# Picked k and v move to the edge values' PSUM bank, and the units of picks run on across groups

## The chip, the cores and the metric

The kernel runs on one core of a Trainium2 chip. The metric is device time in microseconds (us), from one launch. Five engines work beside each other, each through its own instructions in order: PE (TensorE, matmuls; its weight loads are shown as PEld), DVE (VectorE), ACT (ScalarE), POOL (GpSimd, which here issues the gathers) and SP (SyncE, which here issues the other DMAs). They wait for each other by semaphores. [...]

## The reference

6,250 nodes with 64 values each, 206,250 edges sorted by destination, one edge attribute of 64 values for each edge:

```python
Qh = (x @ Wq.T + bq).reshape(n, H, D)          # H = 4 heads, D = 16
Kh = (x @ Wk.T + bk).reshape(n, H, D)
Vh = (x @ Wv.T + bv).reshape(n, H, D)
Ee = (edge_attr @ We.T + be).reshape(-1, H, D)
score = (Kh[src] * Qh[dst] * (1.0 / np.sqrt(D)) * Ee).sum(-1)
score = jnp.exp(jnp.clip(score, -5.0, 5.0))
msg = Vh[src] * score[..., None]
wV = jax.ops.segment_sum(msg, dst, num_segments=n)
out = layernorm(x + wV)
```

So each edge needs k and v of its source, q of its destination and its own edge values; then messages are summed by destination.

## The kernel before

**Tiles and groups.** 128 edges are a tile, 8 tiles a group, and there are 202 groups (`NG`). A prologue (about the first 100 us) makes the tables of q, k and v in HBM. Then the loop `for g in range(NG + 1)` does one group in each iteration, with the parts of several groups in flight: edge values of group g+3, queries of g+2, the transposed product of g+1, and scores and messages of g.

**k and v of the sources.** Most tiles get k and v by an indirect DMA from the table (`gather_kv`, L295, on POOL, one for each tile). For the last two tiles of four groups out of five they are picked by PE instead. A batch is four such tiles, 512 edges: PE multiplies x by one-hot columns, in 13 units (`UNITS`). A unit is four matmuls of 128 x 512, two into each of the PSUM banks `px[0]` and `px[1]`; the thirteenth is two. So a batch is 50 matmuls (`picks`). There are 78 batches, and both banks belong to one batch at a time: they accumulate over its 13 units. The one-hot columns come from DVE (`hots`, L696) for pieces of two units; for three pieces of seven, DVE makes them in bf16 and ACT widens them (`widened`, L707). They are made in the iteration ahead of the one that uses them, into six buffers.

**The end of a batch.** When its last unit is done, DVE masks both banks into SBUF (`picked`, `xs[0]` and `xs[1]`, L722 and L723). Only then may the next batch's first unit write `px`. In the iteration after, ACT fills the bank `rooms` with the bias (`biased_kv`, L733), PE multiplies `xs` by the weights into it (`picked_kv`, 8 products, 16 records), and ACT copies it to the tiles' places among k and v (`place_kv`, L739, two copies). `rooms` is the bank `qq`, into which PE also writes the queries of a group (`queries`) and which DVE's `terms` (L769) reads.

**The edge values' bank.** PE writes the edge values of group g+3 into `ee` at the end of iteration g (`edges`, 2 matmuls, the group `room<-et,we_sb` of the profile); ACT adds the bias and copies them to SBUF early in iteration g+1 (`biased`, L755). `ee` is one half of a PSUM tile `room` of two banks. The other half holds `pa`, the sums of the messages (PE `sums`, the group `room<-msg`; read by DVE's `add`, L900), and `folded` (PE `fold_blocks`, read by `add_blocks`, L957).

**Which iteration does what.** Batches take three and two iterations in turn (`LENGTHS = [3, 2]`), so the loop repeats after five. I call them places 1 to 5: g = 1, 6, 11, ... is place 1. A batch's units never pass its own iterations: places 1 to 3 do 4, 4 and 5 units of one batch, places 4 and 5 do 6 and 7 units of the next. A batch ends in places 3 and 5 (`READY`), and `picked` stands at the very end of DVE's work there; biases, products and copies of k and v follow in places 4 and 1.

**Order within an iteration**, by engine, as written out by hand:

- PE: two units of picks; the transposes of g+1 (`turn`, L775, needs `terms` of g+1); then `queries` of g+2, or in places 4 and 1 `picked_kv` instead; the rest of the units with the sums (every other iteration) and folds between them; in places 4 and 1 `queries` only here, behind `place_kv`; `edges`.
- DVE: `products` (L806, L808), `terms` of g+1, `add`, `add_blocks`, one piece's `hots`, `message` (L830), the other pieces, the one-hot rows of the sums (L792), `take` (L850), in places 3 and 5 `picked`, then some layer norm.
- ACT: `weigh` (L813, L815), in places 4 and 1 `biased_kv`, `biased` of g+2, a copy of the messages (L844), widening, the one-hot columns of the queries (L272, L278), in places 4 and 1 `place_kv`; `sources` (L257 and L258, with L259 on DVE) turns a batch's source numbers into what `hots` compares.
- SP: the loads, with `fetch_sources` (L252, 256 KB into one buffer) among those of edges, queries and keys.
- POOL: 6 or 8 gathers, each behind a mark in PE's order.

What follows are the functions that the change touches, with the line numbers of the profile.

## Time and profile before

| | |
|---|---|
| median of 3 runs | 1998.6 us (1994.48 to 2001.87) |
| the profiled execution | 2019.47 us, span 2017.7 us |
| PE busy | 1738.5 us, 86% of the span |
| DVE busy | 1486.0 us, 74% |
| ACT busy | 1328.1 us, 66% |
| POOL busy | 1255.5 us, 62% |
| granted TensorE clock, mean | 0.932 |
| picks on PE | 3900 matmuls, 1143.6 us busy, 115.5 us idle before them |
| gathers on POOL | 1260, mean 965 ns |

Read it so: no engine is busy all the time, and PE is busiest. Matmuls overlap in their pipeline, so PE's busy time is not time at its peak rate, and the mean of one matmul is longer than the distance from its start to the next one's. The granted clock is the share of full speed at which TensorE was allowed to run. Idle time counts only on the engine that sets the pace; the rows that tell for whom PE waited are therefore the first to read.

### The profile page before, as it was taken

Reading aid. Unit: us, or ns where it says so; the run is one execution under the profiler, and the core shown is the slowest. Engines: PE = TensorE matmul, PEld = TensorE weight load, DVE = VectorE, ACT = ScalarE, POOL = GpSimd, SP = SyncE. Lnnn points to the kernel's source line nnn. Section 1 sums busy time; section 2 is a strip of 40 time slices with the busy share of each in tenths; the row PEclk is TensorE's granted clock in tenths of the full one; section 3 lists DMA queues with packets and bytes.
Section 4 is the critical chain, followed back from the end, with each engine's and each line's share of the span. In section 5 each row is a group of like instructions: output and inputs, shape, how many; then the busy total and the mean of one; then the engine's idle time right before and its main releaser. Section 6 shows DMA issues by size and latency. Waiting matters only on the chain.

```text
span 2017.7 us, 25692 instructions
## 1 busy us (share of the span) xinstructions
PE 1738.5 (86%) x7993; PEld 1259.1 (62%) x7993; DVE 1486.0 (74%) x2650; ACT 1328.1 (66%) x2047; POOL 1255.5 (62%) x1310
## 2 busy tenths in 40 slices
PE   6569989888888898979888989888888988889995
PEld 6346666666666665657566666666666666656664
DVE  5457777777777686878777777778777777678786
ACT  3456676676766676767667667667766667577674
POOL 6566666666666665666666666666666666666441
PEclk9789999999999998999899999999989999999996
DMA  6523333333333333333333333333333333333320
GB/s 178 190 90 114 100 103 103 98 97 100 93 108 101 91 102 88 102 115 99 93 97 92 107 104 93 104 90 103 101 88 114 104 95 104 97 93 98 97 71 20
DMA packets 116116, 203.70 MB, mean 101 GB/s; under 512 B 54784, under 2 KB 56425, under 8 KB 115855
## 3 DMA queue, kind: packets, MB, share of 16 engines
q1 hardware_dynamic: 73932, 116.94, 19.0%
q0 software_dynamic: 41600, 83.97, 14.7%
q10 hardware_dynamic: 436, 1.04, 0.2%
q8 instruction: 65, 1.06, 0.2%
q14 instruction: 83, 0.68, 0.1%
HBM read 194.25 MB, written 7.59 MB: 100 GB/s over the span
## 4 chain that ended last, share of the span: by engine, by line
PE 63%; DVE 16%; issue 7%; ACT 6%; another core or an unknown queue 4%; DMA 2%; POOL 1%; DVEq 0%; SPq 0%; ACTq 0%; POOLq 0%
PE pick L744 37%; PE room L744 10%; PE qq L744 10%; PE qe L775 4%; DVE hot L696 3%; DMA kv<-kv_tab,src_i 2%; DVE score L808 2%; DVE prod L806 1%; DVE qe L830 1%; DVE x L722 1%; DVE term L769 1%; POOL kv L295 1%; ACT kv L739 1%; DVE msg L850 1%
## 5 line engine op out<-in xcount | busy, mean ns | idle before, releaser
L295 POOL DMA_INDIRECT kv<-kv_tab,src_i x1260 | 1216.2, 965 | 708.8 <-issue 277.1
L744 PE MATMUL pick<-hot,parts 128*128 128x512 f32 x3900 | 1143.6, 436 | 115.5 <-DVE x L722 79.5
L744 PEld LDWEIGHTS pick<-hot,parts 128*128 128x128 f32 x3900 | 742.3, 198 | 418.8 <-issue 167.8
L696 DVE TENSOR_TENSOR hot<-from,still 128x1024 fp32r<-128x1024 bf16 x231 | 280.3, 1213 | 0.6 <-ACT from L257 0.6
L707 ACT ACTIVATE hot<-thin 128x1024 fp32r<-128x1024 bf16 x234 | 245.4, 1049 | 19.4 <-remote 19.3
L769 DVE TENSOR_TENSOR term<-eb,qq 128x512 f32<-128x512 f32 x202 | 137.3, 680 | 137.2 <-PE qq L744 98.1
L755 ACT ACTIVATE eb<-room,be_col 128x512 f32<-128x512 f32 x202 | 137.1, 679 | 148.2 <-DVE still L900 50.4
L744 PE MATMUL room<-et,we_sb 128*128 128x512 f32 x404 | 226.2, 642 | 7.5 <-ACT eb L755 6.2
L844 ACT ACTIVATE msg<-qe 128x512 fp32r<-128x512 f32 (+1 forms) x206 | 123.2, 598 | 157.5 <-DVE qe L830 74.4
L278 ACT ACTIVATE to<-to,one_p 126x1024 bf16<-126x1024 bf16 x198 | 225.7, 1140 | 0.1
L272 ACT ACTIVATE to<-kb,minus_row 126x1024 bf16<-126x1024 uint8 x198 | 225.2, 1137 | 0.0
L813 ACT ACTIVATE score<-score,five_p 128x32 f32<-128x32 f32 x203 | 64.1, 316 | 235.4 <-DVE score L808 144.6
L775 PE MATMUL qe<-ident,term 128*128 128x128 f32 x806 | 135.5, 294 | 58.9 <-DVE term L769 39.4
L775 PEld LDWEIGHTS qe<-ident,term 128*128 128x128 f32 x806 | 104.0, 151 | 111.9 <-DVE term L769 55.8
L744 PE MATMUL qq<-w,x 128*128 128x128 f32 x1248 | 165.8, 288 | 5.0 <-issue 3.6
L806 DVE TENSOR_TENSOR prod<-kv,qe 128x512 f32<-128x512 f32 x203 | 137.0, 675 | 43.1 <-remote 38.3
L830 DVE SCALAR_TENSOR_TENSOR qe<-weight,kv 128x512 f32<-128x512 f32 x200 | 139.8, 699 | 35.1 <-ACT weight L815 22.3
L722 DVE SCALAR_TENSOR_TENSOR x<-odd,upper,pick 128x512 f32<-128x512 int32 x77 | 57.3, 744 | 144.7 <-PE pick L744 115.2
L744 PEld LDWEIGHTS qq<-w,x 128*128 128x128 f32 x1248 | 155.6, 202 | 12.9 <-issue 8.0
L696 DVE TENSOR_TENSOR thin<-from,still 128x1024 bf16<-128x1024 bf16 x231 | 157.1, 680 | 0.0
L808 DVE TENSOR_REDUCE score<-prod 128x32 f32<-128x512 f32 x203 | 138.5, 682 | 7.0
L850 DVE TENSOR_TENSOR msg<-qe,msg 128x512 fp32r<-128x512 f32 x194 | 132.2, 681 | 2.9 <-ACT msg L844 1.4
(166 smaller groups left out, 1490.5 us busy)
## 6 DMA issues: line engine op xcount, KB each, us to landing
et<-in_eT SPq DMA_DIRECT2D x100, 512.0 KB
kb<-key_tab SPq DMA_DIRECT2D x101, 252.0 KB
kv<-kv_tab,src_i POOLq DMA_INDIRECT x1260
srcs<-in_src_rows SPq DMA_DIRECT2D x78, 256.0 KB
qw<-q_tab SPq DMA_DIRECT2D x202, 15.8 KB
kv_tab<-kv_sb SPq DMA_DIRECT2D x4, 640.0 KB
q_tab<-q SPq DMA_DIRECT2D x5, 480.0 KB
out<-y SPq DMA_DIRECT2D x2, 512.0 KB
```

The costliest lines, as they stand in the source:

```text
L272: nc.scalar.activation(TO[g][:, :n, :], KB.pop(g)[:, :n * P].rearrange("p (j e) -> p j e", j=n), AF.Square, bias=minus_row3[:3 * W])
L278: nc.scalar.activation(TO[g][:, :n, :], TO[g][:, :n, :], AF.Relu, bias=one_p[:3 * W], scale=-1.0)
L295: return nc.gpsimd.indirect_dma_start(out=kv_of(g)[:, j, :], out_offset=None, in_=kv_tab[:, :], in_offset=bass.IndirectOffsetOnAxis(ap=src ...
L696: nc.vector.tensor_tensor(to.rearrange("p b (a c) -> p b a c", c=2), pairs((FROM if hi < UNITS else OVER)[m])[:, None].to_broadcast(shape) ...
L707: nc.scalar.activation(*THIN.pop(0), AF.Copy)
L744: mark.append(nc.tensor.matmul(*aps, **kw))
L769: nc.vector.tensor_mul(TERM[g][:, :n], EB.pop(g)[:, :n], qq[:, :n])
L775: nc.tensor.transpose(qe[g % 2][:, 2 * k:2 * k + 2, :], TERM[g][:, k, :], ident)
L806: nc.vector.tensor_mul(prod, kv_of(g)[:, lo:hi, :C], qe[g % 2][:, lo:hi, :])
L808: nc.vector.tensor_reduce(SCORE[g], prod.rearrange("p g (h d) -> p g h d", h=H), axis=AX.X, op=OP.add)
L830: nc.vector.scalar_tensor_tensor(to.rearrange("p g (h d) -> p g h d", h=H), WEIGHT.pop(g)[:, :, :, None].to_broadcast([P, n, H, D]), LEAST ...
L850: nc.vector.tensor_sub(part_of(g, 1)[1], left, part)
```

## The change

Three things change together.

1. **The bank of k and v.** `ee` and `room` become two tiles of one bank each, in place of one tile of two banks. `rooms`, where k and v of a batch are made, is now `ee` and no longer `qq`. So `queries` of g+2 takes its place in the middle of every iteration, and it is `edges` of g+3 that comes behind `place_kv` in places 4 and 1. `biased_kv` moves behind `biased` on ACT, since it now overwrites what `biased` reads.
2. **Units run on.** The units of all batches are one stream, cut in 4, 6, 6, 4, 6 for places 1 to 5 (one more in the very first). A batch's end lies within an iteration: in place 3 the first two units are its last ones (`head`), and four of the next batch follow; in place 5 the first five are its last ones, and one of the next batch follows. PE's order there is: the head (with `turn` behind the head of two, or after the second unit of the head of five), `queries`, sums and folds, `edges`, and only then the next batch's units. `picked` moves forward on DVE: in place 3 it stands behind `add` and `add_blocks`, ahead of the `hots` and of `message`; in place 5 behind `message` and all `hots`, ahead of the one-hot rows and `take`.
3. **Sources.** `fetch_sources` and `sources` come one iteration earlier, since the next batch's first pieces are needed earlier. In the iteration of a batch's end, its `sources` for the batch after next follow `picked`.

Work is neither added nor removed: as many matmuls, copies and DMAs as before.

```diff
--- before.py
+++ after.py
@@ -97,13 +97,27 @@
 READY = [begin(m + 1) - 1 for m in range(LAST)]
 
 
+FLOW = 4, 6, 6, 4, 6
+STREAM = [(m, p, u) for m in range(LAST) for p, piece in enumerate(PIECES) for u in range(*piece)]
+UPTO = [0] * (LEAD + 1)
+for g in range(LEAD, NG):
+    UPTO.append(UPTO[-1] + FLOW[(g - LEAD) % len(FLOW)] + (g == LEAD))
+assert UPTO[NG] >= len(STREAM)
+assert all(UPTO[r] < (m + 1) * UNITS <= UPTO[r + 1] for m, r in enumerate(READY))
+
+
+def units_of(g):
+
+    return STREAM[UPTO[g]:UPTO[g + 1]] if g < NG else []
+
+
 def pieces_of(g):
 
-    for m in range(LAST):
-        if BEGIN[m] <= g <= READY[m]:
-            n, k = READY[m] - BEGIN[m] + 1, g - BEGIN[m]
-            return [(m, p) for p in range(len(PIECES) * k // n, len(PIECES) * (k + 1) // n)]
-    return []
+    return [(m, p) for m, p, u in units_of(g) if u == PIECES[p][0]]
+
+
+SOURCES = {LEAD: 1, **{r: m + 2 for m, r in enumerate(READY)}}
+FETCHES = {r - 1: m + 2 for m, r in enumerate(READY)}
 
 
 PICKED = [(r + k, r + k + 1) for r in READY for k in [min(4, NG - 2 - r - 1)]]
@@ -663,17 +677,17 @@
             nc.tensor.transpose(col, row_b[:, 0:1].to_broadcast([P, P]), ident_b)
             nc.tensor.transpose(still[:, C:C + UNITS].bitcast(BF16),
                                 half_b[:2 * UNITS].to_broadcast([2 * UNITS, P]), ident_b[:2 * UNITS, :2 * UNITS])
-            room = fixed.tile([P, 2, 4 * P], F32, name="room")
-            ee = room[:, 0].rearrange("p (i e) -> p i e", e=P)
-            pa = room[:, 1, :2 * PA]
-            folded = room[:, 1, 2 * PA:2 * PA + 2 * C].rearrange("p (b c) -> p b c", c=C)
+            ee = fixed.tile([P, G // 2, P], F32, name="ee")
+            room = fixed.tile([P, 4 * P], F32, name="room")
+            pa = room[:, :2 * PA]
+            folded = room[:, 2 * PA:2 * PA + 2 * C].rearrange("p (b c) -> p b c", c=C)
             sum_ = still[:, 2 * P:2 * P + C]
             px = [fixed.tile([P, 4 * P], F32, name=f"pick{k}") for k in range(2)]
             xs = [accp.tile([P, 4 * P], F32, name=f"x{k}") for k in range(2)]
             qq = fixed.tile([P, G // 2, P], F32, name="qq")
             qe = [fixed.tile([P, G, C], F32, name=f"qe{k}") for k in range(2)]
 
-            rooms = qq.rearrange("p i e -> p (i e)").rearrange("p (j c) -> p j c", j=BATCH)
+            rooms = ee.rearrange("p i e -> p (i e)").rearrange("p (j c) -> p j c", j=BATCH)
 
             def pairs(ap):
 
@@ -1013,7 +1027,9 @@
             widened()
             for g in range(NG + 1):
                 now, before = g < NG, g > 0
-                todo, ahead = [(m, p, u) for m, p in pieces_of(g) for u in range(*PIECES[p])], pieces_of(g + 1)
+                todo, ahead = units_of(g), pieces_of(g + 1)
+                ending = READY.index(g) if g in READY else None
+                head = [one for one in todo if one[0] == ending]
                 going, where = [], []
                 if g == 0:
                     going = alone(lots(4))
@@ -1025,8 +1041,8 @@
                     nc.sync.dma_start(dst_c[:, :min(KEYS, T - t)], dst[:, t:min(t + KEYS, T)])
                 if g % LG == 0 and g + 3 * LG < NG:
                     fetch_edges(g // LG + 3, work, 3)
-                if g + 1 in BEGIN[1:]:
-                    fetch_sources(BEGIN.index(g + 1) + 1, work)
+                if g in FETCHES:
+                    fetch_sources(FETCHES[g], work)
                 if g + 4 < NG:
                     fetch_queries(g + 4)
                 if g % 2 == 0 and g + 6 < NG:
@@ -1052,10 +1068,15 @@
                     add(s)
                 if g - 1 in FOLDS:
                     add_blocks(FOLDS[g - 1])
+                if 0 < len(head) <= 3:
+                    for one in head:
+                        picks(*one)
+                        where.append(mark[-1])
+                    picked(ending)
+                if g + 2 < NG:
+                    biased(g + 2)
                 if g - 1 in READY:
                     biased_kv(READY.index(g - 1))
-                if g + 2 < NG:
-                    biased(g + 2)
                 for piece in ahead[:1]:
                     hots(*piece)
                 if now:
@@ -1082,31 +1103,48 @@
                         short += [lambda lo=lo: sums(s, slice(lo, lo + 4)) for lo in range(0, G, 4)]
                     else:
                         short.append(lambda: sums(s))
-                for k in range(max(len(todo), 3)):
+                for k, one in enumerate(head if len(head) > 3 else []):
+                    picks(*one)
+                    where.append(mark[-1])
+                    if k == 1 and g + 1 < NG:
+                        turn(g + 1)
+                if head:
+                    if len(head) <= 3 and g + 1 < NG:
+                        turn(g + 1)
+                    if g + 2 < NG:
+                        queries(g + 2)
+                    while short:
+                        short.pop(0)()
+                    if g + 3 < NG:
+                        edges(g + 3)
+                    if len(head) > 3:
+                        picked(ending)
+                    for one in todo[len(head):]:
+                        picks(*one)
+                        where.append(mark[-1])
+                for k in range(0 if head else max(len(todo), 3)):
                     for one in todo[k:k + 1]:
                         picks(*one)
                         where.append(mark[-1])
                     if k == 1:
                         if g + 1 < NG:
                             turn(g + 1)
+                        if g + 2 < NG:
+                            queries(g + 2)
                         if g - 1 in READY:
                             picked_kv(READY.index(g - 1))
                             place_kv(READY.index(g - 1))
-                        elif g + 2 < NG:
-                            queries(g + 2)
-                    if k in (2, 4) and short and g not in READY:
+                    if k in (2, 4) and short:
                         short.pop(0)()
                 while short:
                     short.pop(0)()
-                if g + 2 < NG and g - 1 in READY:
-                    queries(g + 2)
-                if g + 3 < NG:
+                if g + 3 < NG and not head:
                     edges(g + 3)
                 where.append(mark[-1])
                 if g + 4 < NG:
                     onehot_rows_rest(g + 4)
-                if g in BEGIN:
-                    sources(BEGIN.index(g) + 1, *from_odd())
+                if g in SOURCES:
+                    sources(SOURCES[g], *from_odd())
                 for i, lot in enumerate(going):
                     gather((lot, where[i * len(where) // len(going)]))
                 for h in ([g] if g < NG - 3 else []) + ([g + 1] if NG - 4 <= g < NG - 1 else []):
@@ -1122,8 +1160,6 @@
                         widen(s)
                 if parted:
                     take(g, 0)
-                if g in READY:
-                    picked(READY.index(g))
                 if done:
 
                     while closed < B - 2 and summed[closed] <= g:
```

## The prediction

> **What bounds the kernel now.** I read the page first: span, busy times, and the chain that ended last.
>
> ```profile
> span 2017.7 us, 25692 instructions
> PE 1738.5 (86%) x7993; PEld 1259.1 (62%) x7993; DVE 1486.0 (74%) x2650; ACT 1328.1 (66%) x2047; POOL 1255.5 (62%) x1310
> PE 63%; DVE 16%; issue 7%; ACT 6%; another core or an unknown queue 4%; DMA 2%; POOL 1%; DVEq 0%; SPq 0%; ACTq 0%; POOLq 0%
> L295 POOL DMA_INDIRECT kv<-kv_tab,src_i x1260 | 1216.2, 965 | 708.8 <-issue 277.1
> ```
>
> PE sets the pace, but only 63% of the chain is its work. So I ask for whom PE waits, and read the view of waits (line, releaser: us in total, times, longest), PE's rows first, then four of DVE and ACT.
>
> ```profile
> PE pick L744 <- DVE x L722: 79.5, 23, 6.0
> PE qq L744 <- ACT kv L739: 44.0, 32, 4.4
> PE qe L775 <- DVE term L769: 39.4, 22, 12.3
> PE pick L744 <- issue: 35.1, 37, 2.5
> ...
> DVE x L722 <- PE pick L744: 115.2, 42, 5.1
> DVE term L769 <- PE qq L744: 98.1, 50, 5.1
> ...
> ACT eb L755 <- DVE still L900: 50.4, 20, 6.5
> ACT eb L755 <- DVE y L957: 40.1, 13, 7.4
> ```
>
> The first row is the end of a batch: PE has nothing to do until DVE has emptied `px`. Next I cut the loop into cycles of five iterations, at the ends of place 5's edge matmuls. The windows' columns are us, busy us (and instructions) of PE, PEld, DVE, ACT and POOL, granted clock, DMA share, GB/s. The first row is all 39 cycles, the others single ones.
>
> ```profile
> 103.60:1971.70 1868.10, 1647.44 (x7684) 1191.61 (x7683) 1404.04 (x2413) 1265.25 (x1898) 1186.21 (x1231) 0.94 0.34 99
> 977.80:1024.40 46.60, 41.80 (x200) 31.14 (x199) 35.21 (x61) 32.68 (x49) 30.44 (x32) 0.93 0.37 108
> 1838.10:1887.00 48.90, 41.97 (x197) 30.05 (x197) 36.85 (x67) 32.80 (x49) 31.31 (x33) 0.97 0.37 110
> 1887.00:1928.70 41.70, 40.33 (x198) 29.53 (x197) 35.81 (x61) 31.58 (x48) 14.04 (x15) 1.00 0.26 77
> ```
>
> A cycle takes 1868.1 / 39 = 47.9 us, PE is busy for 42.2 of it, and the clock is below full speed. One late cycle has next to no stall and a clock of 1.00: 41.7 us. It also has half the gathers (15 against 33), so it shows what PE can do, not what the whole kernel can. Then the timeline around an end of a batch in place 3 (start, us, what, idle time before it), with the same work undisturbed in the late cycle behind it.
>
> ```profile
> 992.23 1.02 PE L744 MATMUL room<-et,we_sb 128*128 128x512 f32 x2
> ...
> 992.73 0.68 DVE L769 TENSOR_TENSOR term<-eb,qq 128x512 f32<-128x512 f32 x1
> ...
> 995.98 0.64 DVE L900 TENSOR_REDUCE still<-room 64x64 f32<-64x128 f32 x2 [2.56 <-PE qq L744]
> ...
> 996.71 0.69 ACT L755 ACTIVATE eb<-room,be_col 128x512 f32<-128x512 f32 x1 [2.77 <-DVE still L900]
> ...
> 997.04 1.21 DVE L696 TENSOR_TENSOR hot<-from,still 128x1024 fp32r<-128x1024 bf16 x1
> 997.38 0.95 POOL L295 DMA_INDIRECT kv<-kv_tab,src_i  x1 [0.30 <-issue]
> 998.25 1.02 PE L744 MATMUL room<-et,we_sb 128*128 128x512 f32 x2
> ...
> 1000.62 0.68 DVE L792 TENSOR_TENSOR of<-still,key 128x1024 bf16<-128x1024 bf16 x1
> 1001.22 0.68 DVE L850 TENSOR_TENSOR msg<-qe,msg 128x512 fp32r<-128x512 f32 x1
> ...
> 1001.82 0.74 DVE L722 SCALAR_TENSOR_TENSOR x<-odd,upper,pick 128x512 f32<-128x512 int32 x1
> 1002.47 0.74 DVE L723 SCALAR_TENSOR_TENSOR x<-odd,upper,pick 128x512 f32<-128x512 int32 x1
> ...
> 1002.61 3.78 PE L744 MATMUL pick<-hot,parts 128*128 128x512 f32 x8 [3.34 <-DVE x L722]
> 1006.19 1.05 PE L775 MATMUL qe<-ident,term 128*128 128x128 f32 x4
> 1007.04 2.48 PE L744 MATMUL qq<-w,x 128*128 128x128 f32 x16
> ...
> 1015.03 0.41 PE L744 MATMUL qq<-to,qw 126*64 126x512 bf16 x2
> ...
> 1019.06 4.48 PE L744 MATMUL pick<-hot,parts 128*128 128x512 f32 x18
> ...
> 1909.40 2.43 PE L744 MATMUL pick<-hot,parts 128*128 128x512 f32 x8
> 1911.92 0.66 PE L775 MATMUL qe<-ident,term 128*128 128x128 f32 x4
> 1912.62 2.05 PE L744 MATMUL qq<-w,x 128*128 128x128 f32 x16
> ...
> 1926.74 1.11 PE L744 MATMUL room<-msg,wide 128*128 128x256 f32 x8
> ```
>
> Three things are to be seen. DVE reaches `picked` at 1001.82 though PE had done its last matmul of the iteration by about 999.3: DVE lost 2.56 us in `add` and then had hots, message, one-hot rows and `take` ahead of it. ACT's copy of the edge values stood behind DVE's `add` (2.77 us): `ee` and `pa` are halves of one tile, and the order kept is the tile's. And after 3.34 us of idling PE does the same work in 7.31 us (3.78 + 1.05 + 2.48) instead of 5.14 (2.43 + 0.66 + 2.05).
>
> **The change part by part**, against the profiled execution, 2019.5 us (span and 1.8 us around it), 1% above the median of 1998.6. The 39 cycles have 78 ends of batches.
>
> *(a) The wait for `px`.* In place 3 the head is 6 matmuls, 1.5 us at 4.48 / 18 = 0.25 us each. Ahead of the next batch's first unit PE then has transposes (0.66), queries (0.41), sums (1.11, every second iteration, so 0.55) and edges (1.02): 2.6 us. DVE's two masks take 1.4. In place 5 the cover behind the head is 2.0 us, as the transposes lie within it. So the wait goes: -79.5. Bounds: 0, if DVE is late again, and -114.6 with the 35.1 of the same matmuls without a named releaser.
>
> *(b) The slow stretch behind it.* 7.31 - 5.14 = 2.2 us for each of 23 stalls: -50. Bounds: 0, if other idling takes its place, and -0.06 x 1868 = -112, if the clock (0.94) becomes full. [...]
>
> *(c) Queries out of k and v's way.* DVE's `terms` waited 98.1 us for queries that came late; most of that hits places 2 and 5, of which PE felt a part in its wait for `term`: 39.4 less 12.3 at the loop's start leaves 27. I take half: -13 (bounds 0 and -27). PE's own wait of 44.0 for ACT's copies does not go: edges stand where queries stood. ACT's queue ahead of the copies loses its wait for `terms` and keeps the rest, so I take 0. Bounds: -44, and +65, if all 78 waits cost the mean of 44.0 / 32 = 1.4 us (109 - 44).
>
> *(d) `ee` in a tile of its own.* ACT's copy no longer waits for `add` and `add_blocks`, 90.5 us in two rows. That is idling of ACT, which delays widened hots; PE pays what it waits at picks without a named releaser, at most 35.1. Half: -18 (bounds 0 and -35).
>
> *(e) `picked` in the middle of DVE's queue.* This is the added wait: DVE now waits for the head. Behind it in place 3 stand two pieces' hots, the message, one-hot rows, `take`; ACT's message copy, PE's sums and the next iteration's picks wait for those. If DVE comes 1.3 us too late, or PE's signal does, the cover of 2.6 - 1.4 = 1.2 is used up. The 2.56 us above shows such lateness; I take 0.65 us for 39 places: +25 (bounds 0 and +50). In place 5 DVE goes on 5.1 us (18 x 0.25 + 0.6) into the iteration and has two masks, the source numbers, one-hot rows and `take` left, about 3.0 us, against 3.1 of PE: it begins place 1 level with PE instead of ahead, and the transposes there wait some 0.5 us for `term`: +20 (bounds 0 and +100, 2.56 for each).
>
> *(f) At nothing.* Units moved between iterations leave DVE's hots and PE's picks as many. The moved `sources` are 1.4 us on ACT (two of 0.72) in places 3 and 5, where `place_kv` is not. The early fetch of sources goes past queries, keys and edges in SP's queue by one iteration; those are ordered four to six iterations ahead, and PE waited for a DMA of them once, 2.1 us. If that cover went, each late set of queries would stop PE as that one did.
>
> Sum: -79.5 - 50 - 13 - 18 + 25 + 20 = -115.5. So 1904 in such an execution, and 1904 x 1998.6 / 2019.5 = **1884 us** as a median.
>
> ```profile
> PE qq L744 <- DMA kb<-key_tab: 2.1, 1, 2.1
> ...
> L257 ACT ACTIVATE from<-srcs,from_row x77: 707/720/727, 109.6 to 1937.0; 128x512 bf16<-128x512 int32 x77
> ```
>
> **The rivals.**
>
> *A: all stalls go.* Units of 4, 6, 6, 4, 6, with k and v's products in the places of 4, give each iteration about 8 us of PE, and DVE has 36 us of work in a cycle. If PE then runs as in the late cycle, 39 x (47.9 - 41.7) = 242 us go: 2019.5 - 242 = 1778, as a median **1759**. Against it: that cycle had half the gathers. POOL needs 0.965 us for one and 0.30 between two, 32 in a cycle: 40.5 us. It would be busy nearly all the time, and all engines share one pace. A middle between A and the sum, 1800 to 1830, is quite possible.
>
> *B: the wait moves.* Edges wait for ACT's copies at every batch (+65 in (c)), place 5 costs its middle (+50), and the clock stays low, as PE still idles once in a cycle (b is 0): -79.5 - 13 - 18 + 25 + 50 + 65 = +30, or +5 with half of (b)'s gain: as a median **2003**. [...] For B: the wait's place on PE is the same. Against: `biased_kv` starts earlier.
>
> *C: slower, DVE stuck at the head.* PE's signal at a head reaches DVE late, and all that stands behind `picked` is late for PE. Priced at L per end of a batch, it replaces the +45 of (e): -115.5 - 45 + 78 L. It loses from L = 2.1 us; with the 2.56 of the timeline it is +39, as a median **2037**. For it: in place 3 `add` waited until 995.98 for matmuls on `room` whose last had ended by 993.25. Against: DVE already waits for PE's last pick in 42 of 78 batches (115.2 us), and PE stopped for `x` in only 23.
>
> **How the numbers follow.** The sum's case has 0.59, A 0.20, B 0.08, C 0.13. The forecast is 1884. Its own range takes the bounds as independent: the roots of their summed squares are 92 us below the sum and 143 above, of which I use two thirds, 1823 to 1979. The range that holds 8 in 10 is 1775 to 2005: below it lies part of A, above it C and part of B. A measurement of this kernel can tell about 0.5%, 10 us, from no change. Faster is the sum's case and A, 0.79; about the same is B, 0.08; slower is C, 0.13.
>
> **What would show it.** (a) is right if PE's waits for `x` at L722 fall from 79.5 to under 20 us. (b): a mean clock near 0.97 or more in the loop, and 8 picks at about 2.4 us at each batch's start. (c): DVE's waits of `term` for `qq` gone, and a new row of PE's `edges` waiting for ACT's `kv` of 20 to 60 us. (d): no row of ACT's `eb` behind L900 or L957. (e): DVE's `x` waiting for picks in the middle of places 3 and 5, with transposes behind `term` at place 1. A is right if a cycle takes under 43 us and POOL hardly idles. B shows as edges behind `kv` of over 100 us. C shows as long idling of PE for `hot`, `term` and `x` behind a DVE that waits at L722. I am wrong at the root if PE's idling in place 4 stays at 3 us with L722 out of it.

## The result and the profile after

The changed kernel takes 2017.4 us (median of 4 runs, 2016.2 to 2022.1), the kernel before 1999.2 (4 runs): a ratio of 1.0092, 95% interval 1.0069 to 1.0114. The forecast was 1884 and faster. The profiled execution of after took 2022.1 us, that of before 2019.5.

The page of after (span and busy times), then windows cut as the prediction cut those of before, at the ends of place 5's edge matmuls: all 39 cycles, a single one, and the last full one. The columns are as in the prediction.

```profile
span 2020.3 us, 25628 instructions
PE 1719.7 (85%) x7993; PEld 1257.5 (62%) x7993; DVE 1483.9 (73%) x2650; ACT 1330.0 (66%) x2047; POOL 1247.3 (62%) x1310
```

```profile
103.10:1973.80 1870.70, 1633.21 (x7684) 1192.90 (x7683) 1402.21 (x2412) 1267.76 (x1898) 1177.62 (x1230) 0.95 0.35 98
930.20:978.00 47.80, 42.31 (x204) 30.43 (x203) 34.45 (x60) 35.03 (x52) 30.47 (x33) 0.96 0.35 97
1931.80:1973.80 42.00, 39.79 (x207) 29.27 (x205) 33.25 (x58) 28.90 (x45) 20.16 (x21) 1.00 0.25 69
```

A cycle takes 1870.7 / 39 = 48.0 us, as before (47.9). PE is busy for 41.9 of it instead of 42.2, and the clock is 0.95 instead of 0.94. So PE does its work a little faster and idles a little more. The late cycle with fewer gathers (21) again takes 42 us.

Where PE idles is told by the groups of its instructions (busy us, mean ns of one, idle us just before them, and for whom). First the six groups of the loop in the kernel before, then in after.

```profile
L744 PE MATMUL pick<-hot,parts 128*128 128x512 f32 x3900 | 1143.6, 436 | 115.5 <-DVE x L722 79.5 <-issue 35.1
L744 PE MATMUL room<-et,we_sb 128*128 128x512 f32 x404 | 226.2, 642 | 7.5 <-ACT eb L755 6.2 <-issue 1.2
L744 PE MATMUL qq<-w,x 128*128 128x128 f32 x1248 | 165.8, 288 | 5.0 <-issue 3.6
L775 PE MATMUL qe<-ident,term 128*128 128x128 f32 x806 | 135.5, 294 | 58.9 <-DVE term L769 39.4 <-DVE score L808 10.2 <-issue 8.8
L744 PE MATMUL room<-msg,wide 128*128 128x256 f32 x776 | 117.9, 284 | 2.7 <-issue 1.8 <-ACT eb L755 0.8
L744 PE MATMUL qq<-to,qw 126*64 126x512 bf16 x396 | 83.9, 418 | 48.5 <-ACT kv L739 44.0 <-issue 2.3 <-DMA kb<-key_tab 2.1
```

```profile
L758 PE MATMUL pick<-hot,parts 128*128 128x512 f32 x3900 | 1118.3, 432 | 33.1 <-issue 17.6 <-DVE x L736 13.4 <-DVE x L737 1.7
L758 PE MATMUL ee<-et,we_sb 128*128 128x512 f32 x404 | 229.5, 651 | 88.8 <-ACT kv L753 50.2 <-issue 25.8 <-ACT eb L769 12.7
L758 PE MATMUL ee<-w,x 128*128 128x128 f32 x1248 | 182.5, 306 | 64.7 <-ACT ee L747 28.3 <-issue 19.7 <-ACT eb L769 16.6
L789 PE MATMUL qe<-ident,term 128*128 128x128 f32 x806 | 127.9, 282 | 63.7 <-DVE term L783 37.4 <-issue 17.8 <-DVE score L822 4.2
L758 PE MATMUL room<-msg,wide 128*128 128x256 f32 x776 | 123.9, 292 | 2.3 <-issue 2.3
L758 PE MATMUL qq<-to,qw 126*64 126x512 bf16 x396 | 82.0, 408 | 1.8 <-issue 1.8
```

The idle time before picks fell by 82 us, as forecast, and that before queries by 47. It came back before edges (+81), before the products of k and v (+60) and before transposes (+5). The six groups' sum went from 238 to 254 us: +16. PE's busy time fell by 19 us meanwhile, and the profiled executions are 2.6 us apart (the medians 18).

The last view of after is its timeline in one place 4, here at 766 to 781 us (start, us, what, idle time before it and its releaser).

```profile
767.73 0.95 POOL L309 DMA_INDIRECT kv<-kv_tab,src_i  x1 [0.31 <-issue]
768.22 0.60 ACT L747 ACTIVATE ee<-bkv_all 128x512 f32<-128x512 f32 x1
...
768.87 2.05 PE L758 MATMUL ee<-w,x 128*128 128x128 f32 x16 [0.98 <-ACT eb L769]
...
768.98 0.94 POOL L309 DMA_INDIRECT kv<-kv_tab,src_i  x1 [0.30 <-issue]
...
770.23 0.95 POOL L309 DMA_INDIRECT kv<-kv_tab,src_i  x1 [0.30 <-issue]
...
770.68 2.11 PE L758 MATMUL pick<-hot,parts 128*128 128x512 f32 x8
...
771.48 0.95 POOL L309 DMA_INDIRECT kv<-kv_tab,src_i  x1 [0.30 <-issue]
...
772.73 0.94 POOL L309 DMA_INDIRECT kv<-kv_tab,src_i  x1 [0.30 <-issue]
...
773.98 0.94 POOL L309 DMA_INDIRECT kv<-kv_tab,src_i  x1 [0.30 <-issue]
...
776.56 0.66 ACT L753 ACTIVATE kv<-ee 128x256 f32<-128x256 f32 x2 [4.24 <-remote]
776.80 0.94 POOL L309 DMA_INDIRECT kv<-kv_tab,src_i  x1 [1.88 <-remote]
...
777.28 2.08 PE L758 MATMUL ee<-et,we_sb 128*128 128x512 f32 x2 [4.49 <-ACT kv L753]
...
778.36 3.46 PE L758 MATMUL pick<-hot,parts 128*128 128x512 f32 x8
```

PE had ended the products at 770.92 and its picks at 772.79. ACT, with nothing else to do, began to copy k and v only at 776.56, and POOL was released at nearly the same time. The profile names no releaser for either ("remote"), but the copies wait for semaphores of PE and of ACT itself alone: ACT had waited for PE's signal, which came 5.6 us after the work. In those microseconds POOL had issued gathers back to back, the last one ending at 774.92. PE stood idle for 4.49 us, and did the next eight picks at half speed (a granted clock of 0.5 until 780.57; 3.46 us instead of 2.1). The experiments take the chain of k, v and edges first, and then this.

### The profile page after: what moved, and what is told of

Same layout as the page of the kernel before. It is cut to its first block, busy times and chain, and to the rows that moved or that the text cites. A ratio compares the mean times of both kernels' runs of the same rounds, so it can differ in the third digit from the quotient of the medians.

```text
span 2020.3 us, 25628 instructions
## 1 busy us (share of the span) xinstructions
PE 1719.7 (85%) x7993; PEld 1257.5 (62%) x7993; DVE 1483.9 (73%) x2650; ACT 1330.0 (66%) x2047; POOL 1247.3 (62%) x1310
## 5 line engine op out<-in xcount | busy, mean ns | idle before, releaser
L758 PE MATMUL pick<-hot,parts 128*128 128x512 f32 x3900 | 1118.3, 432 | 33.1 <-issue 17.6
L758 PE MATMUL ee<-et,we_sb 128*128 128x512 f32 x404 | 229.5, 651 | 88.8 <-ACT kv L753 50.2
L758 PE MATMUL ee<-w,x 128*128 128x128 f32 x1248 | 182.5, 306 | 64.7 <-ACT ee L747 28.3
L769 ACT ACTIVATE eb<-ee,be_col 128x512 f32<-128x512 f32 x202 | 136.2, 674 | 152.2 <-PE qq L758 50.8
L758 PEld LDWEIGHTS ee<-w,x 128*128 128x128 f32 x1248 | 166.2, 215 | 86.6 <-ACT ee L747 38.0
L736 DVE SCALAR_TENSOR_TENSOR x<-odd,upper,pick 128x512 f32<-128x512 int32 x77 | 57.5, 747 | 175.6 <-PE pick L758 48.8
L789 PE MATMUL qe<-ident,term 128*128 128x128 f32 x806 | 127.9, 282 | 63.7 <-DVE term L783 37.4
L914 DVE TENSOR_REDUCE still<-room 64x64 f32<-64x128 f32 x194 | 57.9, 298 | 127.9 <-PE room L758 44.5
L758 PEld LDWEIGHTS ee<-et,we_sb 128*128 128x128 f32 x404 | 66.7, 198 | 122.3 <-ACT kv L753 61.9
```

Of the source, the lines that this page charges most:

```text
L758: mark.append(nc.tensor.matmul(*aps, **kw))
L769: nc.scalar.activation(EB[g][:, :n], ee[:, :n], AF.Identity, bias=be_col)
L789: nc.tensor.transpose(qe[g % 2][:, 2 * k:2 * k + 2, :], TERM[g][:, k, :], ident)
```

## Experiments: the bank, the flow, and the chain behind them

Kernels that are compared ran on one chip, with the kernel before beside them. The chips differ, so each is named by a letter, with the median of the kernel before: A 1999.1, B 2023.3, C 2017.6 (and 2017.3 at another time), D 1786.5, E 2015.6 us. Ratios are to the kernel before on the same chip.

**The bank alone** (chip A), on the kernel before:

```diff
-            room = fixed.tile([P, 2, 4 * P], F32, name="room")
-            ee = room[:, 0].rearrange("p (i e) -> p i e", e=P)
+            ee = fixed.tile([P, G // 2, P], F32, name="ee")
+            room = fixed.tile([P, 4 * P], F32, name="room")
-            rooms = qq.rearrange("p i e -> p (i e)").rearrange("p (j c) -> p j c", j=BATCH)
+            rooms = ee.rearrange("p i e -> p (i e)").rearrange("p (j c) -> p j c", j=BATCH)
```

with `biased` ahead of `biased_kv` and queries ahead of `picked_kv`, as in the changed kernel.

> The kernel before with the bank alone moved: k and v of picked nodes are formed in the edge values' bank, which has a tile of its own, with queries ahead of the products; units of picks, the place of `picked` and the end of the iteration stay as in the kernel before. Theory 1 (the stall moved with the bank): PE still waits for `x` (some 80 us), no longer 44 us at queries but some 50 to 65 at edges behind ACT's `kv`, and 20 to 30 at the k,v products behind `biased_kv`; so not faster than before, 2000 to 2040 us. Theory 2 (PE stops about once in a cycle whatever it stops for): within 10 us of the kernel before, 1990 to 2010, with PE's idle time per cycle unchanged at 5.5 to 6.1 us.

Measured: 2002.3 us, 1.0009 (0.9984 to 1.0034). It lies in the ranges of both theories, but PE waits more for `x` than before (110.7 us) and little for the products, which speaks for theory 2. The bank by itself, with `ee` in its own tile, is worth nothing on this chip.

**The flow alone** (chip A), on the changed kernel:

```diff
-            rooms = ee.rearrange("p i e -> p (i e)").rearrange("p (j c) -> p j c", j=BATCH)
+            rooms = qq.rearrange("p i e -> p (i e)").rearrange("p (j c) -> p j c", j=BATCH)
```

with `biased_kv` ahead of `biased` and, in places 4 and 1, queries behind `place_kv`.

> The changed kernel with k and v back in the queries' bank, queries behind ACT's copies in places 4 and 1 as in the kernel before; units still run on across batches. Theory 1: the wait for `x` stays at 10 to 20 us, the wait of edges for `kv` (50.2) goes, that of queries (44.0 in the kernel before) comes back; with the clock's share 1900 to 1960. Theory 2: the stall of place 4 shows at the queries or at `term` instead, 2000 to 2030.

Measured: 2017.3 us, 1.0092 (1.0063 to 1.0121). PE waits 16.4 us for `x`, but 72.2 at queries for ACT's `kv` (44.0 in the kernel before) and 35.3 at the products. That is theory 2's range. With the flow of units, whatever bank is used, the idle time that leaves `px` turns up in the chain of k and v, and the flow alone shows the whole loss. The products' row with the bank alone, then with the flow alone:

```profile
L744 PE MATMUL ee<-w,x 128*128 128x128 f32 x1248 | 165.7, 287 | 13.7 <-issue 6.5 <-ACT eb L755 3.7 <-ACT ee L733 2.9
L758 PE MATMUL qq<-w,x 128*128 128x128 f32 x1248 | 176.6, 301 | 48.3 <-ACT qq L747 35.3 <-issue 5.4 <-ACT score L827 3.6
```

**No k and v** (chip A):

```diff
-                if g - 1 in READY:
+                if g - 1 in READY[:6]:
                     biased_kv(READY.index(g - 1))
```

and the same for `picked_kv` and `place_kv`.

> The changed kernel without biased_kv, picked_kv and place_kv from the seventh batch on (the picked tiles' k and v are left out: 72 of 78 batches lose 16 products of 2.05 us in all on PE and three operations of 1.26 us on ACT). Theory 1: with the work (72 x 2.05 = 148 us) go the waits at edges and products (some 80 us) and the half-speed stretch behind them (2.4 us in a cycle, some 90 us): 1700 to 1780. Theory 2: only PE's work goes, 1860 to 1880.

Measured: 1976.5 us, 0.9875 (0.9828 to 0.9921), outside both ranges. With 148 us of PE's work and the chain itself gone, only 41 us went against the changed kernel's 2017.4. PE idled more, and again for `x` and `term`, as the view of waits shows:

```profile
PE pick L758 <- DVE x L736: 81.5, 34, 8.3
PE qe L789 <- DVE term L783: 65.6, 36, 8.6
PE qe L789 <- issue: 62.6, 37, 7.0
```

So on such a chip PE's work does not set the pace, which was where the prediction's working began.

**The chain earlier** (chip A): `biased` and `biased_kv` at the head of the iteration, the products behind the first unit, `place_kv` on ACT ahead of the widened hots and the one-hot rows.

```diff
+                if g - 1 in READY:
+                    biased(g + 2)
+                    biased_kv(READY.index(g - 1))
                 if former:
                     keep(g - 1, 1)
...
+                if g - 1 in READY:
+                    for one in todo[:1]:
+                        picks(*one)
+                        where.append(mark[-1])
+                    started = 1
+                    picked_kv(READY.index(g - 1))
+                    place_kv(READY.index(g - 1))
                 widened()
```

> The changed kernel with the k,v chain begun earlier in places 4 and 1: ACT's `biased` and `biased_kv` at the head of the iteration, ahead of `weigh`; the products behind the first unit of picks instead of the second, ahead of transposes and queries; `place_kv` on ACT ahead of the widened hots and the one-hot rows. Theory 1: the waits at edges (50.2) and at products (28.3) fall to under 30 together and part of the half-speed stretches with them: 1900 to 1960. Theory 2: PE stops in place 4 for something else, 2000 to 2030.

Measured: 2025.9 us, 1.0121 (1.0056 to 1.0187). The wait of edges for `kv` fell from 50.2 to 0.4 us, but the products, standing earlier, wait 110.7 us for `biased_kv`. The stall moved by one link. The time lies in theory 2's range, but that theory names no cause.

## Experiments: the gathers

The timeline above, with PE's signal 5.6 us behind the work, suggested a cause: PE's signals are late while POOL issues gathers.

**No gathers**, the changed kernel and the kernel before (chip B):

```diff
-                elif g + 1 < NG and step_of[g + 1] + KVB - 1 < NS:
+                elif g + 1 < NG and step_of[g + 1] + KVB - 1 < 2 * KVB:
                     going = lots(step_of[g + 1] + KVB - 1)
```

> The changed kernel without the loop's gathers of k and v from the sixth buffer round on (POOL's L309, some 1000 of 1260 left out; the nodes' k and v of an earlier use stay in the buffers). Leaving out 148 us of PE's work and the k,v chain won only 40 us, so something else sets the pace. Theory 3 (the gathers make PE's signals late, which is where DVE, ACT and PE lose their time): PE's waits in the loop nearly vanish, the clock is full and a cycle takes what the late cycle with half the gathers took, 41 to 42 us: 1740 to 1790. Theory 4 (a ring of dependencies between DVE, ACT and PE sets the pace, the gathers beside it): 1970 to 2020.

> The kernel before with the same gathers left out. Theory 3: 1750 to 1830, and the changed kernel without gathers ahead of it by at least the 30 us that its units and bank were predicted to win without the clock. Theory 4: 1970 to 2010.

Measured: 1836.8 us (0.9079, 0.9022 to 0.9136) and 1833.9 us (0.9065, 0.9005 to 0.9124). Both are above theory 3's ranges, the second by 4 us, but 187 us went with work that lies on another engine; theory 4 is out. And without gathers the change is worth nothing: the two differ by 0.2%, and the changed kernel is not the 30 us ahead that theory 3 had it. PE's waits, first of the kernel before, then of the changed one, both without gathers:

```profile
PE qe L775 <- DVE term L769: 57.2, 54, 7.1
PE qq L744 <- ACT kv L739: 25.7, 20, 1.5
PE pick L744 <- DVE x L722: 18.8, 20, 3.6
```

```profile
PE ee L758 <- ACT ee L747: 53.7, 51, 2.5
PE qe L789 <- DVE term L783: 45.6, 36, 6.0
PE ee L758 <- ACT kv L753: 18.2, 20, 1.8
```

Of the 79.5 us for `x` only 18.8 remain without gathers; the other 60 went with them. The change takes 17 of the 18.8 away, and pays 53.7 at the products for `biased_kv`.

**Plain loads instead of gathers** (chip C), and **half of the gathers** (chip C):

```diff
-            ins = gather_kv(g, j)
+            ins = (gather_kv if place_of(g)[0] < 2 * KVB else load_kv)(g, j)
...
+        return nc.sync.dma_start(kv_of(g)[:, j, :], kv_tab[t * P:(t + 1) * P, :])
```

```diff
+                    going = going[::2] if step_of[g + 1] + KVB - 1 >= 2 * KVB else going
```

> The changed kernel with the gathers from the sixth buffer round on turned into plain loads of as many rows and bytes, issued by SP (rows in order instead of the listed ones, so k and v are wrong). Without these gathers 180 us went. Theory 3a (POOL's issuing of gathers, back to back at 0.95 us and 0.30 between, holds back PE's signals): the same gain, 1830 to 1870. Theory 3b (the traffic of the data, 100 against 65 GB/s, does it): 1980 to 2030.

> The changed kernel with every second gather of the loop left out from the sixth buffer round on (k and v of an earlier use stay in those places). Theory 3a with POOL near its limit (32 gathers x 1.25 us in a cycle of 47.9): with 16 a cycle POOL runs few gathers in a row, signals are late by over 1 us far less often, and most of the gain is there, 1830 to 1880. If each gather costs the same by itself: half of the gain, 1920 to 1940.

Measured: 1837.4 us (0.9109, 0.9083 to 0.9136) and 1841.8 us (0.9131, 0.9104 to 0.9158). Both are in theory 3a's ranges. The same bytes by SP cost nothing (1837.4 us, against 1836.8 without the gathers on B), so it is not the amount of traffic; the loads took rows in order, so POOL's issuing is not told apart from the reading of scattered rows. And half of the gathers cost next to nothing (1841.8 us), so it is not so much per gather.

What may count is how many stand in a row. For each product of PE that raises its semaphore (after 200 us) I took from the trace the time from its end to the next recorded change of that semaphore, and sorted by the number of the gather, in a row with less than 0.5 us between two, that was going on. Share with over 1 us, and in the last two rows the same for the semaphores of DVE and ACT:

```
kernel (chip)               no gather   1st, 2nd   3rd, 4th   5th and later
before                          9%         11%        28%         68%
after                           6%         13%        27%         53%
after, half the gathers (C)     0%          4%        14%      too few
before, even release (E)        6%         12%        36%         57%
before, even release (D)        0%          0%         0%          0%
after, even release (D)         0%          0%         0%          0%
before, DVE's semaphore         9%         10%        30%         40%
before, ACT's semaphore        19%         13%        31%         56%
```

The last two rows are a warning. The recorder loses changes: in the kernel before there are 1717 for 2167 instructions of PE that raise the semaphore and 1288 for 2456 of DVE, with even release on D 2549 for 2552. A lost change counts here as a late one, so the shares are upper bounds, and their order may be that of the losses. What shows late signals is the engine that waits. DVE's and ACT's signals come in time whatever is recorded: in all 203 iterations of before and after, ACT starts `weigh` at most 0.04 us after it is free and DVE's score has ended, and DVE its message at most 0.03 us after ACT's weights. PE's signals don't. In so many of the 78 batches ACT stood idle for over 1 us after the last product's end before it began to copy k and v (in before, after, with one mark, with DVE's marks and on E, each of these waits is for PE's semaphore and ACT's own alone):

```
                              before   after
as they are                     32       34
no gathers (B)                   3        2
plain loads by SP (C)                     3
half of the gathers (C)                   3
one mark, below (B)                      48
DVE's marks, below (C)                   42
even release, below (E)         23
even release, below (D)          0        0
```

**One mark for all gathers of an iteration** (chip B), and **DVE's instructions of the iteration as marks** (`steps`, chip C):

```diff
-                    gather((lot, where[i * len(where) // len(going)]))
+                    gather((lot, where[0]))
```

```diff
-                    gather((lot, where[i * len(where) // len(going)]))
...
+                for i, lot in enumerate(going):
+                    gather((lot, (steps or mark[-1:])[i * max(len(steps), 1) // len(going)]))
```

> The changed kernel with all gathers of an iteration held behind one mark of PE, that of the iteration's start, instead of marks spread over it: POOL issues them back to back and waits far less for PE. Theory 3: the lag of PE's signals lies in the first 8 x 1.27 = 10 us of an iteration whatever it was, so time within 20 us of the changed kernel, 2000 to 2040. A theory 5 (POOL's many waits on PE's marks are what burdens PE's signals): faster, 1850 to 1950.

> The changed kernel with the gathers held behind DVE's instructions of the iteration, evenly, instead of PE's, so that POOL no longer stands on signals that are late themselves. Theory 3a with pauses that only let the signals through: POOL's pauses come as DVE goes on, and if DVE is not held itself the runs of gathers get shorter: 1920 to 1990. If the waits on PE's late signals are what keeps POOL from running on (as with one mark for all, 2136): 2050 to 2150. Theory 4 (a ring of dependencies apart from the gathers): 2017.

Measured: 2135.8 us (1.0526, 1.0460 to 1.0593) and 2269.8 us (1.1248, 1.1220 to 1.1275), both above every range. A row has 8.8 gathers on the mean with one mark (5.3 in after). With DVE's marks the mean is 6.3 and up to 18 stand in a row (13 in after), and ACT waits over 1 us at the copies in 48 and 42 batches (34 in after). It seems that PE's own marks, late as they are, had limited the rows: a POOL that stands on a late signal issues nothing (1.88 us before the gather at 776.80 in the first timeline).

**The early chain without gathers** (chip C); the edits of "The chain earlier" and "No gathers" together.

> The early k,v chain (`biased` and `biased_kv` at the head of the iteration, products behind the first unit, `place_kv` ahead of widened hots and one-hot rows) without the loop's gathers. With signals prompt, PE still waited 53.7 us for `biased_kv` and 18.2 us for `kv` there (1836.8 us). Theory 1 (the change moved the stall into this chain): both go, 1765 to 1800. Theory 4: 1825 to 1845.

Measured: 1883.2 us (0.9336, 0.9308 to 0.9364), above both ranges and 46 us more than with the chain where the change has it (chip B). The wait for `kv` went, the one for `biased_kv` rose from 53.7 to 126.9. Theory 1's remedy was wrong even without gathers: PE comes to the products before ACT has written the bias.

**Other releases of the gathers**, two groups, three groups, and a mark two places later, on the kernel before, and two groups on the changed kernel (all on chip C):

```diff
-                    gather((lot, where[i * len(where) // len(going)]))
+                    gather((lot, where[i * 2 // len(going) * len(where) // 2]))
```

```diff
+                    gather((lot, where[min(i * len(where) // len(going) + 2, len(where) - 1)]))
```

> The kernel before with an iteration's gathers released in two groups, at its start and at its middle mark, instead of one by one. Theory 3a, run length: a run of 3 or 4 gathers leaves most signals prompt (of those that end during a run's first two gathers about 1 in 10 is over 1 us late, during the fifth and later 6 in 10 or more), so runs of 4 with a pause between win: 1940 to 1985. Theory 6, POOL's own time: 32 gathers of 1.25 us take 40 of 47.9 us and a pause longer than 1.3 us per 6 gathers isn't to be had; runs join up again, 1985 to 2030.

> The kernel before with an iteration's gathers released in three groups. Theory 3a: between the kernel before and the one with two groups, 1950 to 1995. Theory 6: no difference, 1990 to 2010.

> The kernel before with each gather held behind a mark two places later, so that POOL stands closer behind PE and stops sooner when PE's signals are late. Theory 3a: shorter runs, 1940 to 1990. Theory 6: POOL loses one to two us at each iteration's start and never has them to spare, 2010 to 2080.

> The changed kernel with the gathers in two groups per iteration. Theory 3a: 1950 to 2000. Theory 6: 2005 to 2050. Either way it stands to the kernel before with two groups as the changed kernel stands to the kernel before, within 1%, if the change's own worth is nothing.

Measured: 2116.7 us (1.0499, 1.0481 to 1.0518), 2050.3 (1.0149, 1.0121 to 1.0177), 2033.3 (1.0071, 1.0053 to 1.0089), 2109.0 (1.0463, 1.0382 to 1.0544). All are slower and above theory 3a's ranges; the third lies in theory 6's, the others above that too. With two groups most rows have 3, 6, 9 or 11 gathers, and their mean rises from 5.7 to 6.7 (before) and from 5.3 to 7.0 (after). With three groups and with the later mark the mean falls (5.4 and 5.0), and the time grows all the same. So the length of rows alone does not order these times, and no order of release tried here gained any. The changed kernel is within 0.4% of the kernel before here too.

**An even release**, one gather per 1.24 us of PE's work, on both kernels (chip D), and on the kernel before once more (chip E):

```diff
+                for k in range(k0, len(mark)):
+                    work += cost[k]
+                    if pend and work >= due:
+                        gather((pend.pop(0), mark[k]))
+                        due = max(due, work - 1.24) + 1.24
```

> The kernel before with each gather released by its own product of PE, one for every 1.24 us of PE's work (0.25 us for a pick, 1.02 for edges, 0.13 for the rest), evenly over the whole loop instead of over the marks of an iteration, two of which coincide at its start. With two groups an iteration the runs got longer (9 and 11 gathers instead of 5 to 7) and the time grew by 5%. If the length of runs is what counts and the even release shortens them: 1940 to 1990. If POOL at 1.25 us a gather then never pauses of itself, the signals come only when POOL stands on a late one: 2000 to 2060.

> The changed kernel with the same even release. By the first reading 1940 to 2000, by the second 2010 to 2070; the changed kernel within 1% of the kernel before, with even release in both, if the change's own worth is nothing.

> The same kernel as e16_even_b once more, since on the chip of that run no signal of PE was over 1 us late even in rows of 50 gathers and more, and the kernel before itself took 1786 us there. If this chip has late signals (the kernel before at about 2000 us), the open reading is decided here: 1940 to 1990 if the even release shortens the runs of gathers, 2000 to 2060 if POOL then never pauses of itself. If it has none (before at 1786 us): 1780 to 1795 again, and nothing is decided.

Measured on chip D: 1786.6 us (1.0002, 0.9992 to 1.0012) and 1798.0 (1.0060, 1.0041 to 1.0078); on chip E: 2022.2 (1.0034, 1.0015 to 1.0053). On D the kernel before takes 1786.5 us as it is, so both times there lie below every range and only the last part, the two kernels within 1%, is tested; it holds. On E the time is in the second reading's range, and rows are about as long as before (5.5 against 5.7 on the mean). The timeline of the changed kernel with even release on D, in a row of 12 gathers:

```profile
722.41 0.94 POOL L309 DMA_INDIRECT kv<-kv_tab,src_i  x1 [0.30 <-PE pick L758]
...
723.66 0.94 POOL L309 DMA_INDIRECT kv<-kv_tab,src_i  x1 [0.31 <-issue]
723.79 0.75 DVE L736 SCALAR_TENSOR_TENSOR x<-odd,upper,pick 128x512 f32<-128x512 int32 x1 [1.68 <-PE pick L758]
723.91 0.41 PE L758 MATMUL qq<-to,qw 126*64 126x512 bf16 x2
724.24 1.13 PE L758 MATMUL ee<-et,we_sb 128*128 128x512 f32 x2
...
724.81 3.37 PE L758 MATMUL pick<-hot,parts 128*128 128x512 f32 x12
724.91 0.94 POOL L309 DMA_INDIRECT kv<-kv_tab,src_i  x1 [0.30 <-issue]
```

POOL issues back to back as in the first timeline, and DVE reads `px` as soon as the head's picks are done, queries and edges running meanwhile: what (a) and (e) had drawn. The lateness isn't there. So it depends on the chip (or its condition at that time) and not on gathers alone: on E, with the same kernel before, ACT waited over 1 us at the copies in 23 batches, on D in none. That taking gathers out takes the lateness out was tested on B and C.

D also shows the change with prompt signals. The groups of PE's instructions there, before and after, each with even release:

```profile
L744 PE MATMUL pick<-hot,parts 128*128 128x512 f32 x3900 | 1086.1, 421 | 16.7 <-DVE x L722 16.7
L744 PE MATMUL qq<-w,x 128*128 128x128 f32 x1248 | 159.2, 282 | 1.9
L744 PE MATMUL qq<-to,qw 126*64 126x512 bf16 x396 | 81.5, 406 | 24.9 <-ACT kv L739 24.9
```

```profile
L758 PE MATMUL ee<-et,we_sb 128*128 128x512 f32 x404 | 216.0, 617 | 17.8 <-ACT kv L753 17.5 <-ACT eb L779 0.2
L758 PE MATMUL ee<-w,x 128*128 128x128 f32 x1248 | 181.0, 305 | 53.2 <-ACT ee L747 53.2
```

The change removes 16.7 and 24.9 us and adds 17.6 and 51.3 (53.2 less 1.9): +27 us of idle time, of which 11 show in the time (1798.0 less 1786.6). No version that does the whole work beats the kernel before.

## Why the prediction was wrong, by its steps

- **What bounds the kernel.** "PE sets the pace" fell with the kernel without k and v: 148 us less work for PE, 41 us less time. The late cycle of 41.7 us was a sign of it: the prediction said that it had half the gathers, and took from that a warning on POOL's own time, not on what gathers do to PE's signals. The 2.56 us of `add` behind matmuls that had long ended was quoted, and put down as a chance in (e) and C. Waits of this kind made up most of what PE stood for `x`.
- **(a)** This is the step that failed first. The row came as forecast: PE's wait for `x` fell from 79.5 to 13.4 us. But the step counted the row as time, as if DVE's place in its queue were its cause. Some 60 of the 79.5 hung on the gathers (18.8 remain without them, and 16.7 on D with all of them), and a late signal holds up whatever waits for PE: ACT's idling before `kv` grew from 64.9 to 110.0 us and DVE's before `add` from 87.8 to 127.9, and PE's idling went to edges and products.
- **(b)** -50 forecast. The loop's clock went from 0.94 to 0.95 and not to 0.97; the clock's record has 4.8 us of half speed per cycle instead of 5.4, which is (5.4 - 4.8) / 2 x 39 = 12 us. PE's idling per cycle stayed too (6.1 us instead of 5.7), which was the case for 0 in the bounds.
- **(c)** This is the term that was missing. DVE's wait of `term` for queries is gone, as written. The copies' wait, taken as unchanged, is 50.2 us at edges against 44.0 at queries, in the 20 to 60 named as its sign. But the sum had nothing for the products themselves: PE's idling ahead of them rose from 5.0 to 64.7 us, and on D, where signals are prompt, by 51.3. The bank is the smaller part of it on chip A: with the bank alone, and `biased_kv` behind `biased` as in the change, the row is 13.7 us, with the flow of units alone in the old bank 48.3. PE, which no longer stands at `x` ahead of the products, seems to come to them before ACT is ready; that is argued, and the bank alone was not run on D. "Against: `biased_kv` starts earlier" did not help: PE waited 28.3 us for it.
- **(d)** The rows of ACT's `eb` behind `add` and `add_blocks` are gone, as forecast. The price, -18, did not show: ACT idled 152.2 us before `eb` instead of 148.2, now for PE, and the bank alone, which has this edit in it, ran at 1.0009.
- **(e)** DVE does wait in the middle for the head, but it had waited nearly as long at the end. First the kernel before, then the changed one:

```profile
L722 DVE SCALAR_TENSOR_TENSOR x<-odd,upper,pick 128x512 f32<-128x512 int32 x77 | 57.3, 744 | 144.7 <-PE pick L744 115.2 <-remote 29.5
L736 DVE SCALAR_TENSOR_TENSOR x<-odd,upper,pick 128x512 f32<-128x512 int32 x77 | 57.5, 747 | 175.6 <-PE pick L758 48.8 <-issue 34.8 <-PE ee L758 26.9
```

  That is 31 us more of idle time in front of `picked`. Transposes behind `term` cost 37.4 us (39.4 before), so the forecast +20 there did not come. The rest of the +45 can't be told apart.
- **(f)** As forecast: PE waited for no DMA in the loop.
- **Rivals.** B was the nearest: the wait moved, the clock stayed. Its price, 2003, left out the products' wait, and its sign, over 100 us at edges behind `kv`, did not come (50.2). C had late signals right, but not where they would cost: the 175.6 us are 2.25 for each of 78 ends, above its break-even of 2.1, yet 122.3 of them are there on D with prompt signals, and PE's wait for `term` did not grow. A's cycle of 41.7 us is near the 42.5 (1656.9 / 39) that the kernel before with even release takes on chip D: there POOL's 1186 us of gathers hold nobody up, which the prediction had held against A. That is a matter of the chip, not of the change.

```profile
82.00:1738.90 1656.90, 1570.99 (x7685) 1142.15 (x7683) 1399.98 (x2415) 1260.97 (x1900) 1186.05 (x1235) 0.99 0.40 111
```

- **"Wrong at the root"** was put as PE's idling in place 4 staying at 3 us with L722 out of it. That is what came: 4.49 us in the timeline above, behind `kv`, with PE's idling in a whole cycle as before.

What stays open is why PE's signals are late beside gathers on A, B, C and E and not on D (0 of 78 batches with a wait of over 1 us at the copies), and whether it is the length of rows or POOL's share of busy time that counts. The recorder itself is a suspect: it lost 450 of 2167 changes of PE's semaphore in the kernel before, with late signals, and 3 of 2552 on D (the kernel before, even release), and every time on record comes with its span and clock, so no run here shows the kernel without it.

## What to carry to other kernels

Before a wait is priced, look when its releaser ended. If the signal came microseconds after the work, moving the waiting instruction can move the wait to the next one that needs that engine, and the row that vanishes is no gain by itself (79.5 to 13.4 us at `x` here, with 81 us more before edges). When an engine is freed of a wait, write down every handover that it comes to next (here `biased`, `biased_kv`, products, copies, edges) and give each a term; the one that was left out cost more on D (51.3 us) than the waits that were removed (16.7 and 24.9).

## What the runs showed of the hardware

- Beside POOL's gathers PE's signals came late on four of the five lettered chips and on that of the first result. In the first result ACT stood idle for over 1 us behind the products in 32 (before) and 34 (after) of 78 batches; on B it did so in 48 (one mark), on C in 42 (DVE's marks), on E in 23 (even release), and without gathers, on B, in 3 and 2. On A, with the bank alone, ACT waited 48.1 us in all before the copies of k and v, 40.7 of it with picks or sums of PE named as the releaser, which the copies do not need. In the two handovers counted, in before and after, signals of DVE and ACT came within 0.04 us meanwhile, though the recorder has 1288 of DVE's 2456 changes in before.
- Without the loop's gathers the kernel before took 1833.9 us instead of 2023.3 (B). With the same bytes moved by SP's queue, rows in order, the changed kernel took 1837.4 us (C), as much as without gathers on B (1836.8), and with half of the gathers 1841.8 (C).
- Chips differ: 1786 us on one, 1999 to 2023 on the others, for the same kernel. On the one no batch had such a wait with even release, in rows of 50 gathers and more.
- In the clock's record, which has only 1.0 and 0.5, the time at 0.5 is 0, 3.4, 6.8 or 10.2 us in 38 of the 39 cycles, in before and in after, 5.4 and 4.8 us on the mean of all. On D the mean clock of the 39 cycles was 0.99 (the kernel before, even release).
